# Deformable convolutions and a mixture of experts: where the token rows are normalised, and how often they are stored

## Chip, core and metric

The kernel runs on one core of a Trainium2 chip. Its time is the device time of one execution in microseconds; the time before is 7508.25 us, the median of three runs (7496.17 to 7528.83). The core has five engines with instruction queues of their own: TensorE (PE, with its weight loads PEld), VectorE (DVE), ScalarE (ACT), GpSimd (POOL) and SyncE (SP). SP and POOL issue the transfers here, SP the plain ones and POOL the indirect gathers.

## What is computed

Four images of 256 channels and 64 x 64 pixels, in float32, pass one block of two halves:

```python
# half 1: three deformable 3x3 convolutions on the normalised channels, added to x
x = x + conv3(_ln_c(x))            # each: offsets and mask by a 3x3 convolution,
                                   # 9 taps sampled bilinearly, times the mask, einsum, relu
# half 2: mixture of experts on tokens (a pixel is a token of 256 channels)
t = _to_tokens(x)                  # [4, 4096, 256]
z = (t - mean(t)) / sqrt(var(t) + 1e-5)          # over the channels of a token
probs = softmax(z @ gate_w + gate_b)             # 8 experts, the best two count
t = t + sum over e of cw[:, e] * (gelu(z @ W1[e] + b1[e]) @ W2[e] + b2[e])   # 256 -> 512 -> 256
x = _from_tokens(t)
```

A token goes to two of the eight experts. The kernel sorts the tokens by expert and computes only these.

## The kernel before

**The main work.** A stage is one convolution layer of one image; `run` lists the twelve stages. A stage has 8 blocks of 512 pixels, a block 9 taps. For each tap `samples` (L494) makes POOL gather four tables of corners (L503, 512 KB each, 10 buffers), DVE interpolates (L509, L514) and ACT multiplies by the mask (L517). `turn` transposes two such tiles on PE (L532) and ACT copies the result (L535); `finish` multiplies with the tap's weights (L555). `LAG` keeps the transposes two pairs behind the samples.

**The token path.** After the third layer `tokens` (L587) runs for each of the 32 blocks, cut by `yield` into pieces that are spread over the taps of the next block. It adds x (L599), transposes to tokens (L608, L613), multiplies with the gate (L618), stores the tokens `t` to DRAM (L626, 512 KB), computes mean and 1/sqrt(var) in `normalise` (L62 to L75), normalises the rows on DVE into `z` (L78, four instructions of 128x256), stores `z` (L636, 512 KB) and then ranks the experts (L645 to L686). Row r of a group's `z` table is token r: partition p and quarter t of a block hold token 128 t + p.

**The experts.** Tokens are handled in five groups: images 0, 1 and 2 as a whole, image 3 in two halves. `route` (L690) counts and makes slots, `invert` (L768) makes for each expert slot the number of its token, by a matmul with `self.token`. Then each tile of 256 slots goes through `expert` (L825) in three pieces: (1) `products` of the tile before (DVE adds the bias, L892, and SP stores the result, L895), four transposes of the gathered rows on PE (L840) and a copy on ACT (L844); (2) the first matmul (L856) and the Gelu on ACT (L866); (3) the second matmul (L874). `fetch` (L790) gathers the next tile's expert weights (L800, skipped for a repeated expert) and its token rows `zt` (L812, two gathers of 128 rows); it is called in piece 3, or in piece 2 while `draining`. There are two weight buffers and two buffers for each half of `zt`. There are 163 tiles in all.

**The sums.** `combine_load` (L902) reads tokens back from the `t` store, 128 partitions with two tokens each, `combine_fetch` (L915) gathers the two expert results of a token, `combine` (L930) adds them, weighted, and `give` transposes back and stores the output.

**What sets the order.** Three lanes (`routes`, `tiles`, `sums`) hold pieces with a price in taps. After each tap `pump` gives every lane one tap of credit, and a lane runs the pieces that its credit pays for. An expert tile costs `pace` taps: 5 for the groups of images 0 and 1, 2 for image 2, 1.5 for the first half of image 3, 0 for the second half, each piece a third of it. Where no taps are left, `settle` (between dependent stages and at the end) runs side pieces one by one with `drain(1)` beside each, and the end of `run` calls `drain(3)` until all lanes are empty. `drain(n)` runs n tile pieces and gives the other lanes n/3 and 2n/3 taps. The program's order of instructions is afterwards scheduled per engine ahead of time; `self.after(x)` keeps an instruction behind x in that order, and what has no such ordering may be moved forward to where its inputs are expected.

Of the kernel before, what the change touches and what calls it, by code (L numbers as in the profile page):

```python
# [8 lines left out]
F32 = mybir.dt.float32  # L9
I32 = mybir.dt.int32  # L10
AF = mybir.ActivationFunctionType
ALU = mybir.AluOpType
AX = mybir.AxisListType

P = 128
H = W = 64
C = 256
# [3 lines left out]
TPB = 4  # L21
BLK = P * TPB
NB = H * W // BLK
# [14 lines left out]
GB = 10  # L38
LAG = 2
LEAST = 2.0**-30  # L40
WINN = CC * (RPB + 2) * W
W1N = CC * HID + HC
W2N = HC * C + C
EPS_C = 1e-6
EPS_T = 1e-5
# [72 lines left out]
class Weave:  # L118
# [91 lines left out]

    def ffn_constants(self):
        nc, cst, ins = self.nc, self.cst, self.ins
        self.t_dram = [
            [
                self.dram.tile([P, TPB, C], F32, name=f"t_{b}_{n}", tag=f"t_{b}_{n}")
                for n in range(NB)
            ]
            for b in range(self.B)
        ]
        nf = max(g.NF for g in self.groups)  # L220
        for g in self.groups:
            g.zd = self.dram.tile([g.M * P, C], F32, name=f"z_{g.nm}", tag=f"z_{g.nm}")
        self.ys = [
            self.dram.tile([nf * FT, C], F32, name=f"ys_{i}", tag=f"ys_{i}") for i in range(3)
        ]
        self.gw = cst.tile([P, CC, E], F32, name="gw")
        nc.sync.dma_start(self.gw, ins["gate_w"].rearrange("(c p) e -> p c e", p=P))
        self.gb = cst.tile([P, E], F32, name="gb")
        nc.sync.dma_start(self.gb, ins["gate_b"])

        self.gsum = cst.tile([P, E], F32, name="gsum")

        self.before = cst.tile([P, E, E], F32, name="before")
        nc.vector.memset(self.before, 0.0)
        for e in range(1, E):
            nc.vector.memset(self.before[:, e, 0:e], 1.0)
        self.ones = cst.tile([P, P], F32, name="ones")
        nc.vector.memset(self.ones, 1.0)
        gp = self.ps.tile([P, E], F32, tag="tp", name="gp")
        for c in range(CC):  # L240
            nc.tensor.matmul(
                gp, lhsT=self.ones, rhs=self.gw[:, c, :], start=(c == 0), stop=(c == CC - 1)
            )
        nc.vector.tensor_copy(self.gsum, gp)

        self.upper = cst.tile([P, P], F32, name="upper")
        nc.gpsimd.affine_select(
            self.upper, self.ones, pattern=[[1, P]], base=0, channel_multiplier=-1,
            compare_op=ALU.is_gt, fill=0.0,
        )  # L250

        self.fresh = {}
        for M in {g.M for g in self.groups}:
            fresh = cst.tile([P, E, M], F32, name=f"fresh_{M}")
            nc.vector.memset(fresh, 1.0)
            nc.vector.memset(fresh[:, :, 0:1], 0.0)
            self.fresh[M] = fresh
        part_i = cst.tile([P, 1], I32, name="part_i")
        nc.gpsimd.iota(part_i, pattern=[[0, 1]], base=0, channel_multiplier=1)
        self.part = cst.tile([P, 1], F32, name="part")  # L260
        nc.vector.tensor_copy(self.part, part_i)

        row_i = self.big.tile([P, P], I32, tag="hv", name="row_i")
        nc.gpsimd.iota(row_i, pattern=[[1, P]], base=0, channel_multiplier=0)
        self.row_f = cst.tile([P, P], F32, name="row_f")
        nc.vector.tensor_copy(self.row_f, row_i)
        assert FU * nf <= P
        self.token = cst.tile([P, NB * TPB], F32, name="token")
        nc.vector.tensor_scalar(
            self.token, self.row_f[:, : NB * TPB], float(P), self.part, ALU.mult, ALU.add  # L270
        )


        self.w = None
# [312 lines left out]
    def tokens(self, b, n, r):  # L587

        nc = self.nc
        nm = f"tok_{b}_{n}"  # L590
        grp = next(g for g in self.groups if g.b == b and g.n0 <= n < g.n1)
# [6 lines left out]
        with self.after(self.last):  # L598
            nc.vector.tensor_tensor(r, r, xc, ALU.add)  # L599
        yield  # L600
        tok = self.big.tile([P, TPB, C], F32, tag="b", name=f"t_{nm}")
        z = self.big.tile([P, TPB, C], F32, tag="b", name=f"z_{nm}")
        lg = self.small.tile([P, TPB, E], F32, tag="lg", name=f"lg_{nm}")
        for t0 in range(0, TPB, 2):
            tp = self.ps.tile([P, 2, C], F32, tag="tp", name=f"tp_{nm}_{t0}")
            for t in range(2):
                for o in range(CC):
                    nc.tensor.transpose(  # L608
                        tp[:, t, o * P : (o + 1) * P],
                        r[:, o, (t0 + t) * P : (t0 + t + 1) * P],  # L610
                        self.ident,
                    )
            nc.scalar.copy(tok[:, t0 : t0 + 2, :], tp)  # L613

        lp = self.ps.tile([P, TPB, E], F32, tag="tp", name=f"lp_{nm}")
        for t in range(TPB):
# [6 lines left out]
                    stop=(c == CC - 1),  # L623
                )
        nc.scalar.copy(lg, lp)
        nc.sync.dma_start(self.t_dram[b][n], tok)  # L626
        yield
        rest = normalise(nc, self.small, tok, z, EPS_T, nm)
        with self.after(self.last):
            mean = next(rest)  # L630
            rs = next(rest)
        yield
        with self.after(self.last):
            next(rest, None)
        r0 = (n - grp.n0) * BLK
        nc.sync.dma_start(  # L636
            grp.zd[r0 : r0 + BLK, :].rearrange("(t p) c -> p t c", p=P), z
        )

        def small(tag, shape):  # L640
# [149 lines left out]
    def fetch(self, grp, step):  # L790

        if self.w is None:
            self.w = [
                self.wt.tile([P, 2, WINN], F32, tag="wt", name=f"w_{i}").rearrange(
                    "p a b -> p (a b)"
                )
                for i in range(2)
            ]
        f = grp.order[step]
        self.nc.gpsimd.indirect_dma_start(  # L800
            out=self.w[step % 2][:, : W1N + W2N],
            out_offset=None,
            in_=self.ins["W"],
            in_offset=bass.IndirectOffsetOnAxis(ap=grp.wrow[:, f : f + 1], axis=0),
            bounds_check=E * P - 1,
            oob_is_err=False,
        )
        grp.zt[step] = []
        for u in range(FU):
            zt = self.ffn.tile([P, C], F32, tag=f"zt{u}", name=f"zt_{grp.nm}_{f}_{u}")  # L810
            j = FU * f + u
            self.nc.gpsimd.indirect_dma_start(  # L812
                out=zt,
                out_offset=None,
                in_=grp.zd,
                in_offset=bass.IndirectOffsetOnAxis(ap=grp.tok[:, j : j + 1], axis=0),
            )
            grp.zt[step].append(zt)
# [6 lines left out]
    def expert(self, grp, step):  # L825

        nc = self.nc
        if step == 0:
            self.fetch(grp, 0)
            yield  # L830
        self.products(grp)
        f = grp.order[step]
        nm = f"{grp.nm}_{f}"
        w = self.w[step % 2]
        w1, w2 = w[:, :W1N], w[:, W1N : W1N + W2N]
        zt = grp.zt.pop(step)
        tp = self.ps.tile([P, CC, FT], F32, tag="tp", name=f"ftp_{nm}")
# [61 lines left out]

    def combine_load(self, grp, n, t0):  # L900
        a = self.ffn.tile([P, 2, C], F32, tag="c", bufs=3, name=f"ta_{grp.nm}_{n}_{t0}")
        self.nc.sync.dma_start(a, self.t_dram[grp.b][grp.n0 + n][:, t0 : t0 + 2, :])  # L902
        grp.acc.append(a)

    def combine_fetch(self, grp, m):
# [62 lines left out]
    def begin(self, grp):  # L968
        for step in range(grp.NF):
            gen = self.expert(grp, step)  # L970
            for _ in range(3 + (step == 0)):
                self.tiles.put(grp.pace / 3, lambda gen=gen: next(gen, None))
        self.tiles.put(grp.pace / 3, lambda: self.products(grp))
        self.tiles.put(3, lambda: self.end(grp))

# [36 lines left out]
    def settle(self):  # L1012
        while self.side or self.plans_side:
            for side in (self.side, self.plans_side):
                if side:
                    next(side.pop(0), None)
            if self.tiles.pieces:
                self.drain(1)
        self.draining = False

    def drain(self, pieces):

        self.draining = True
        for _ in range(pieces):
            if self.tiles.pieces:
                self.tiles.pop()
        if self.tiles.pieces:
            self.routes.go(pieces / 3)
            self.sums.go(2 * pieces / 3)
        elif self.routes.pieces:  # L1030
            self.routes.pop()
        elif self.sums.pieces:
            self.sums.pop()

    def run(self):
# [48 lines left out]
                self.finish()  # L1084
                self.settle()
        while self.routes.pieces or self.tiles.pieces or self.sums.pieces:
            self.drain(3)


# [46 lines left out]
```

## Time and profile before

| | |
|---|---|
| median of three runs | 7508.25 us |
| the profiled execution | 7520.62 us, of which the span of instructions is 7518.9 us |
| mean granted TensorE clock | 0.944 |
| PE / DVE / ACT / POOL busy | 86% / 66% / 43% / 60% |
| moved by DMA | 2223.73 MB, 296 GB/s on the mean |
| stages with tokens (third layer of images 0 to 3) | about 1620 to 2110, 3260 to 3850, 5080 to 5650, 6420 to 7090 us |
| experts beside the stages | 2305 to 7090 us, in four groups with pauses |
| end: last routing, last expert tiles, last sums | 7090 to 7519 us |

Lines are read in this way: a group is named by its line, engine, operation and tiles, with its count, its busy time, the mean duration of one, and the idle time of the engine just before it with what ended that. A line of the waits says which instruction sat waiting, and for whom: total time, number of times, the longest. A line of the chain gives the share of each engine in the work that ended last. In a timeline the columns are the start, the duration, engine, line, operation, tiles, the number of instructions merged, and in brackets the idle time ahead.

### The profile page before, as it was taken

To read this page: it belongs to the slowest core of one execution; us is meant where nothing else is said; L and a number is where in the kernel's file an instruction comes from. 1 tells how busy PE (TensorE), PEld (TensorE's weight loads), DVE (VectorE), ACT (ScalarE), POOL (GpSimd) and SP (SyncE) were. 2 spreads that over 40 slices of the span, in tenths; PEclk is the share of its full clock that TensorE was granted. 3 is DMA by queue.
4 is the path that set the end of the run, shared out by engine and by line. 5 is a ranking of instruction groups with operands and counts; after the bars stand their busy time and mean duration, and the time that the engine had idled before them with its cause. 6 is when DMAs were issued, how large, how long until landed. Compare 5 with 4: busy or idle time off the path is not lost.

```text
span 7518.9 us, 88985 instructions
## 1 busy us (share of the span) xinstructions
PE 6443.2 (86%) x26500; PEld 3618.8 (48%) x26500; DVE 4952.9 (66%) x11467; ACT 3266.0 (43%) x7141; POOL 4476.5 (60%) x4245
## 2 busy tenths in 40 slices
PE   6898888888898888889988888888888788977887
PEld 3443333334454444445554445444544555644565
DVE  6776777768887666567777556666768554667421
ACT  3444544445544444445443434444444333444322
POOL 4654666656666565556557656555656565666543
PEclk8999999999999999999999999999999899989998
DMA  8997999989998888888888888888888777888644
GB/s 266 337 325 274 352 342 335 346 331 356 362 349 311 300 305 297 278 315 322 314 293 316 293 280 314 295 302 294 308 306 299 251 271 240 288 302 287 211 139 123
DMA packets 800320, 2223.73 MB, mean 296 GB/s; under 512 B 104729, under 2 KB 302873, under 8 KB 794081
## 3 DMA queue, kind: packets, MB, share of 16 engines
q0 software_dynamic: 551200, 1947.35, 73.3%
q1 hardware_dynamic: 248640, 270.69, 10.9%
q8 instruction: 215, 3.52, 0.2%
q14 instruction: 265, 2.16, 0.1%
HBM read 2160.68 MB, written 196.40 MB: 313 GB/s over the span
## 4 chain that ended last, share of the span: by engine, by line
PE 69%; ACT 10%; issue 7%; another core or an unknown queue 6%; DVE 4%; DMA 2%; POOL 1%; SPq 0%; ACTq 0%; DVEq 0%; POOLq 0%
PE acc L555 34%; PE tp L532 10%; PE ph L856 7%; PE py L874 6%; PE po L357 6%; ACT sT L535 4%; ACT s L517 3%; DVE g L509 2%; DVE s L514 1%; PE pm L371 1%; ACT hT L866 1%; PE ftp L840 1%; ACT win L577 1%; PE tpv L325 1%
## 5 line engine op out<-in xcount | busy, mean ns | idle before, releaser
L503 POOL DMA_INDIRECT g<-tab,idx x3456 | 3685.4, 1066 | 2371.6 <-DVE s L514 1061.8
L555 PE MATMUL acc<-sT,wk 128*128 128x512 f32 x6912 | 3492.1, 620 | 253.4 <-ACT sT L535 147.5
L509 DVE SCALAR_TENSOR_TENSOR g<-g,cf 128x512 f32<-128x512 f32 x3456 | 2559.2, 742 | 269.1 <-DMA g<-tab,idx 245.5
L514 DVE SCALAR_TENSOR_TENSOR s<-g,cf 128x256 f32<-128x256 f32 x3456 | 1662.7, 483 | 1331.3 <-PE tp L532 729.9
L535 ACT COPY sT<-tp 128x512 f32<-128x512 f32 x1728 | 1002.0, 585 | 2312.0 <-PE tp L532 1553.0
L517 ACT ACTIVATE s<-s,cf 128x256 f32<-128x256 f32 x3456 | 1629.5, 508 | 256.7 <-DVE s L514 160.7
L555 PEld LDWEIGHTS acc<-sT,wk 128*128 128x128 f32 x6912 | 1198.9, 198 | 1106.7 <-issue 816.7
L532 PEld LDWEIGHTS tp<-ident,s 128*128 128x128 f32 x6912 | 893.2, 146 | 1666.2 <-issue 898.9
L532 PE MATMUL tp<-ident,s 128*128 128x128 f32 x6912 | 1287.3, 286 | 439.2 <-ACT s L517 253.8
L856 PE MATMUL ph<-fzT,w 128*128 128x256 f32 x2608 | 720.8, 411 | 78.0 <-ACT fzT L844 28.1
L874 PE MATMUL py<-w,hT 128*128 128x256 f32 x2608 | 671.1, 396 | 103.5 <-ACT hT L866 58.0
L856 PEld LDWEIGHTS ph<-fzT,w 128*128 128x128 f32 x2608 | 506.3, 205 | 212.9 <-issue 69.6
L874 PEld LDWEIGHTS py<-w,hT 128*128 128x128 f32 x2608 | 484.5, 196 | 242.0 <-issue 91.9
L866 ACT ACTIVATE hT<-ph,w 128x256 f32<-128x256 f32 x652 | 281.9, 471 | 616.3 <-PE ph L856 378.2
L812 POOL DMA_INDIRECT zt<-z,tok x326 | 333.8, 1024 | 161.5 <-issue 88.0
L800 POOL DMA_INDIRECT w<-in_W,wrow x163 | 178.0, 1092 | 381.2 <-issue 138.8
L357 PE MATMUL po<-win,wo 128*32 128x504 f32 (+1 forms) x2304 | 366.0, 615 | 6.5 <-ACT win L301 4.2
L892 DVE TENSOR_TENSOR y<-py,w 128x512 f32<-128x512 f32 x163 | 111.9, 686 | 341.5 <-PE py L874 285.1
L915 POOL DMA_INDIRECT gy<-ys,slots x256 | 255.6, 998 | 104.5 <-issue 70.0
L930 DVE SCALAR_TENSOR_TENSOR ta<-gy,cw,ta 128x256 f32<-128x256 f32 x256 | 120.6, 480 | 125.6 <-DMA gy<-ys,slots 78.4
L357 PE MATMUL po<-win_pre,wo 128*32 128x504 f32 (+1 forms) x1152 | 184.2, 617 | 2.0 <-ACT om L366 2.0
L366 ACT ACTIVATE om<-po,bo 128x512 f32<-128x512 f32 x96 | 65.9, 687 | 265.3 <-PE po L357 156.3
(154 smaller groups left out, 2961.0 us busy)
## 6 DMA issues: line engine op xcount, KB each, us to landing
tab<-hv SPq DMA_DIRECT2D x512, 128.0 KB
g<-tab,idx POOLq DMA_INDIRECT x3456
ys<-y SPq DMA_DIRECT2D x163, 256.0 KB
tab<-h_pre SPq DMA_DIRECT2D x128, 256.0 KB
wk<-in_conv_w SPq DMA_DIRECT2D x99, 256.0 KB
xc_pre<-in_x SPq DMA_DIRECT2D x32, 512.0 KB
xr_tok<-in_x SPq DMA_DIRECT2D x32, 512.0 KB
t<-t_tok SPq DMA_DIRECT2D x32, 512.0 KB
```

What stands on the lines that cost most here:

```text
L357: nc.tensor.matmul(po[g * Q : (g + 1) * Q, :].rearrange("q (r w) -> q r w", w=W)[:, :, x0:x1], lhsT=self.wo[l][:, 3 * ky + kx, c, :], rhs= ...
L503: self.gathered = nc.gpsimd.indirect_dma_start(out=g.rearrange("p x s f -> p (x s f)"), out_offset=None, in_=self.table(*self.stages[i]), ...
L509: nc.vector.scalar_tensor_tensor(g[:, :, 0, :], g[:, :, 1, :], cf[:, j, 0:1], g[:, :, 0, :], ALU.mult, ALU.add,)
L514: self.last = nc.vector.scalar_tensor_tensor(s, g[:, 1, 0, :], cf[:, j, 1:2], g[:, 0, 0, :], ALU.mult, ALU.add)
L517: nc.scalar.activation(s, s, AF.Copy, scale=cf[:, j, 2:3])
L532: self.turned = nc.tensor.transpose(tp[:, c, u * P : (u + 1) * P], ss[u][:, c * P : (c + 1) * P], self.ident)
L535: nc.scalar.copy(self.sT[:, :, t0 * P : (t0 + 2) * P], tp)
L555: nc.tensor.matmul(acc[:, o, :], lhsT=self.wk[k][:, c, o * P : (o + 1) * P], rhs=sT[:, c, :], start=(k == 0 and c == 0), stop=(k == K - 1 ...
L812: self.nc.gpsimd.indirect_dma_start(out=zt, out_offset=None, in_=grp.zd, in_offset=bass.IndirectOffsetOnAxis(ap=grp.tok[:, j : j + 1], axi ...
L856: nc.tensor.matmul(ph[:, h, :], lhsT=w1[:, o : o + P], rhs=zT[:, c, :], start=(c == 0), stop=(c == CC - 1),)
L866: nc.scalar.activation(ht[:, h, :], ph[:, h, :], AF.Gelu, bias=w1[:, k : k + 1])
L874: nc.tensor.matmul(py[:, u, :], lhsT=hT[h // 2][:, h % 2, u * P : (u + 1) * P], rhs=w2[:, h * C : (h + 1) * C], start=(h == 0), stop=(h == ...
```

## The change

The tokens of a block are stored once, in rows of 258 numbers: 256 channels, then 1/sqrt(var + eps) and -mean/sqrt(var + eps). There is one table per group in place of the `t` tiles and the `z` table. DVE writes the two numbers into the row; the four normalising instructions on DVE and the second store fall away. The row order becomes token 4 p + t, so a partition's four rows are one run of 4128 B, and `self.token` is made by an iota. The expert tiles gather these rows, 1032 B each, and a piece of its own, ahead of the transposes, normalises both halves in place on ACT (Identity with scale and bias per partition); `products` of the tile before moves with the transposes to the piece after it. An expert tile has four pieces in place of three, priced a quarter of `pace` each. `settle` calls `drain(2)`, the end `drain(4)`, and `drain(n)` gives n/4 and 2n/4 taps. `combine_load` reads the first 256 numbers of the rows. The token tile has a tag of its own with one buffer, where `t` and `z` shared two buffers with the pre-blocks' `h`.

```diff
@@ -38,6 +38,7 @@
 GB = 10
 LAG = 2
 LEAST = 2.0**-30
+ROW = C + 2
 WINN = CC * (RPB + 2) * W
 W1N = CC * HID + HC
 W2N = HC * C + C
@@ -210,16 +211,9 @@
 
     def ffn_constants(self):
         nc, cst, ins = self.nc, self.cst, self.ins
-        self.t_dram = [
-            [
-                self.dram.tile([P, TPB, C], F32, name=f"t_{b}_{n}", tag=f"t_{b}_{n}")
-                for n in range(NB)
-            ]
-            for b in range(self.B)
-        ]
         nf = max(g.NF for g in self.groups)
         for g in self.groups:
-            g.zd = self.dram.tile([g.M * P, C], F32, name=f"z_{g.nm}", tag=f"z_{g.nm}")
+            g.td = self.dram.tile([g.M * P, ROW], F32, name=f"t_{g.nm}", tag=f"t_{g.nm}")
         self.ys = [
             self.dram.tile([nf * FT, C], F32, name=f"ys_{i}", tag=f"ys_{i}") for i in range(3)
         ]
@@ -266,9 +260,11 @@
         nc.vector.tensor_copy(self.row_f, row_i)
         assert FU * nf <= P
         self.token = cst.tile([P, NB * TPB], F32, name="token")
-        nc.vector.tensor_scalar(
-            self.token, self.row_f[:, : NB * TPB], float(P), self.part, ALU.mult, ALU.add
-        )
+        token_i = self.big.tile([P, NB, TPB], I32, tag="hv", name="token_i")
+        nc.gpsimd.iota(
+            token_i, pattern=[[BLK, NB], [1, TPB]], base=0, channel_multiplier=TPB
+        )
+        nc.vector.tensor_copy(self.token, token_i.rearrange("p n t -> p (n t)"))
 
 
         self.w = None
@@ -598,8 +594,7 @@
         with self.after(self.last):
             nc.vector.tensor_tensor(r, r, xc, ALU.add)
         yield
-        tok = self.big.tile([P, TPB, C], F32, tag="b", name=f"t_{nm}")
-        z = self.big.tile([P, TPB, C], F32, tag="b", name=f"z_{nm}")
+        tok = self.big.tile([P, TPB, ROW], F32, tag="t", bufs=1, name=f"t_{nm}")
         lg = self.small.tile([P, TPB, E], F32, tag="lg", name=f"lg_{nm}")
         for t0 in range(0, TPB, 2):
             tp = self.ps.tile([P, 2, C], F32, tag="tp", name=f"tp_{nm}_{t0}")
@@ -610,7 +605,7 @@
                         r[:, o, (t0 + t) * P : (t0 + t + 1) * P],
                         self.ident,
                     )
-            nc.scalar.copy(tok[:, t0 : t0 + 2, :], tp)
+            nc.scalar.copy(tok[:, t0 : t0 + 2, :C], tp)
 
         lp = self.ps.tile([P, TPB, E], F32, tag="tp", name=f"lp_{nm}")
         for t in range(TPB):
@@ -623,18 +618,19 @@
                     stop=(c == CC - 1),
                 )
         nc.scalar.copy(lg, lp)
-        nc.sync.dma_start(self.t_dram[b][n], tok)
-        yield
-        rest = normalise(nc, self.small, tok, z, EPS_T, nm)
+        yield
+        rest = normalise(nc, self.small, tok[:, :, :C], None, EPS_T, nm)
         with self.after(self.last):
             mean = next(rest)
             rs = next(rest)
-        yield
-        with self.after(self.last):
-            next(rest, None)
+            nc.vector.tensor_copy(tok[:, :, C], rs)
+            nc.vector.scalar_tensor_tensor(
+                tok[:, :, C + 1], mean, -1.0, rs, ALU.mult, ALU.mult
+            )
+        yield
         r0 = (n - grp.n0) * BLK
         nc.sync.dma_start(
-            grp.zd[r0 : r0 + BLK, :].rearrange("(t p) c -> p t c", p=P), z
+            grp.td[r0 : r0 + BLK, :].rearrange("(p t) c -> p t c", p=P), tok
         )
 
         def small(tag, shape):
@@ -807,12 +803,12 @@
         )
         grp.zt[step] = []
         for u in range(FU):
-            zt = self.ffn.tile([P, C], F32, tag=f"zt{u}", name=f"zt_{grp.nm}_{f}_{u}")
+            zt = self.ffn.tile([P, ROW], F32, tag=f"zt{u}", name=f"zt_{grp.nm}_{f}_{u}")
             j = FU * f + u
             self.nc.gpsimd.indirect_dma_start(
                 out=zt,
                 out_offset=None,
-                in_=grp.zd,
+                in_=grp.td,
                 in_offset=bass.IndirectOffsetOnAxis(ap=grp.tok[:, j : j + 1], axis=0),
             )
             grp.zt[step].append(zt)
@@ -828,6 +824,12 @@
         if step == 0:
             self.fetch(grp, 0)
             yield
+        for zt in grp.zt[step]:
+            nc.scalar.activation(
+                zt[:, :C], zt[:, :C], AF.Identity,
+                scale=zt[:, C : C + 1], bias=zt[:, C + 1 : C + 2],
+            )
+        yield
         self.products(grp)
         f = grp.order[step]
         nm = f"{grp.nm}_{f}"
@@ -899,7 +901,8 @@
 
     def combine_load(self, grp, n, t0):
         a = self.ffn.tile([P, 2, C], F32, tag="c", bufs=3, name=f"ta_{grp.nm}_{n}_{t0}")
-        self.nc.sync.dma_start(a, self.t_dram[grp.b][grp.n0 + n][:, t0 : t0 + 2, :])
+        rows = grp.td[n * BLK : (n + 1) * BLK, :].rearrange("(p t) c -> p t c", p=P)
+        self.nc.sync.dma_start(a, rows[:, t0 : t0 + 2, :C])
         grp.acc.append(a)
 
     def combine_fetch(self, grp, m):
@@ -968,8 +971,8 @@
     def begin(self, grp):
         for step in range(grp.NF):
             gen = self.expert(grp, step)
-            for _ in range(3 + (step == 0)):
-                self.tiles.put(grp.pace / 3, lambda gen=gen: next(gen, None))
+            for _ in range(4 + (step == 0)):
+                self.tiles.put(grp.pace / 4, lambda gen=gen: next(gen, None))
         self.tiles.put(grp.pace / 3, lambda: self.products(grp))
         self.tiles.put(3, lambda: self.end(grp))
 
@@ -1015,7 +1018,7 @@
                 if side:
                     next(side.pop(0), None)
             if self.tiles.pieces:
-                self.drain(1)
+                self.drain(2)
         self.draining = False
 
     def drain(self, pieces):
@@ -1025,8 +1028,8 @@
             if self.tiles.pieces:
                 self.tiles.pop()
         if self.tiles.pieces:
-            self.routes.go(pieces / 3)
-            self.sums.go(2 * pieces / 3)
+            self.routes.go(pieces / 4)
+            self.sums.go(2 * pieces / 4)
         elif self.routes.pieces:
             self.routes.pop()
         elif self.sums.pieces:
@@ -1084,7 +1087,7 @@
                 self.finish()
                 self.settle()
         while self.routes.pieces or self.tiles.pieces or self.sums.pieces:
-            self.drain(3)
+            self.drain(4)
 
 
 def kernel(**inputs):
```

## Prediction

> **What bounds the kernel now.** I read the page from the top: busy shares, then the chain that ended last, then the costliest groups, and after that the waits and the windows of single stages.
>
> ```profile
> PE 6443.2 (86%) x26500; PEld 3618.8 (48%) x26500; DVE 4952.9 (66%) x11467; ACT 3266.0 (43%) x7141; POOL 4476.5 (60%) x4245
> ...
> PE 69%; ACT 10%; issue 7%; another core or an unknown queue 6%; DVE 4%; DMA 2%; POOL 1%; SPq 0%; ACTq 0%; DVEq 0%; POOLq 0%
> ```
>
> TensorE is busy for 86% of the span and holds 69% of the chain. ScalarE has much free time (43% busy), but 10% of the chain; VectorE holds 4% and DMA 2%. Work taken from DVE or DMA is therefore mostly work taken from beside the path, and work given to ACT is partly on it.
>
> The change touches three kinds of stages, and they differ. The windows are: a stage with tokens and the next image's pre-blocks (1630 to 2110), a stretch with experts at pace 2 (5920 to 6340), and the final drain (7390 to 7466). The columns are PE, PEld, DVE, ACT and POOL busy, then the granted clock, DMA share and GB/s.
>
> ```profile
> 1630.00:2110.00 480.00, 422.43 (x1738) 221.19 (x1735) 412.66 (x1113) 241.49 (x529) 302.01 (x275) 0.95 0.96 353
> 5920.00:6340.00 420.00, 375.38 (x1607) 243.56 (x1607) 221.90 (x442) 166.91 (x379) 248.89 (x248) 0.96 0.78 264
> ...
> 7390.00:7466.00 76.00, 72.17 (x328) 58.09 (x326) 6.44 (x10) 19.39 (x45) 16.96 (x18) 1.00 0.29 87
> ```
>
> In the first, PE (88%), DVE (86%) and DMA (96%) are all close to full: here alone is relief of DVE and DMA worth something. In the second DVE and ACT are half idle. In the third PE is 95% busy, one expert tile per 8.2 us (the bias additions of L892 come 8.2 us apart), with ACT 26% busy.
>
> What ends the waits of DVE in the pace-2 stretch:
>
> ```profile
> DVE g L509 <- DMA g<-tab,idx: 130.6, 34, 10.9
> ...
> POOL w L800 <- ACT sT L535: 75.9, 11, 18.2
> ```
>
> POOL holds the weight fetch back (its buffer comes free with L892 two tiles back; in the trace L800 there starts 1.5 us after L892), the tap gathers stand behind it in POOL's queue, and DVE waits for them. One such place, POOL's queue by time:
>
> ```profile
> 6118.46 1.36 POOL L800 DMA_INDIRECT w<-in_W,wrow  x1 [4.07 <-ACT sT L535]
> 6120.12 1.35 POOL L812 DMA_INDIRECT zt<-z,tok  x1 [0.30 <-issue]
> 6121.78 0.98 POOL L812 DMA_INDIRECT zt<-z,tok  x1 [0.30 <-issue]
> ...
> 6125.60 0.95 POOL L503 DMA_INDIRECT g<-tab,idx  x1 [0.30 <-issue]
> ```
>
> The gather issued at 6125.60 is first used at 6129.99 on DVE: 4.4 us from POOL to landing under this load.
>
> **The change, part by part.** The sum is made against the profiled execution, 7520.6 us (span 7518.9); the median shown, 7508, is 12 us below it, and I scale the result by that at the end.
>
> *DVE in the token blocks.* Removed: the normalising group and nothing else on DVE.
>
> ```profile
> L78 DVE TENSOR_SCALAR z_tok<-t_tok,mv_tok,rs_tok 128x256 f32<-128x256 f32 x128 | 45.8, 417 | 0.4
> ```
>
> Added: two 128x4 instructions per block, like L73 at 0.16 us: 64 x 0.16 = 10.2 us. Net -35.6 us of DVE, 1.1 us in each of 32 blocks. Hidden today behind PE in most stages; bounds 0 and -36. The chain of the window 1630 to 2110 gives DVE 9% (L509 4.8, L514 3.9), elsewhere 4%; a quarter of the blocks lies there. The burst also delays the two operations behind it, so I take somewhat more than those shares: **-6 us**.
>
> *Stores, queues of SP and DMA.* One store of 4128 B per partition replaces two of 512 KB; 32 issues of 0.36 us leave SP's queue, where nothing waits for them. The z rows were 1 KB packets: 16384 of them, 50 ns each in the trace's DMA records, over 16 engines 51 us. Given back: the combine loads (L902) read 1 KB runs instead of 2 KB (16384 x 50 ns instead of 8192 x 96 ns, +2 us), and the gathered rows are 1032 B. The gathers of 1 KB rows stand in the records as 4 KB packets (four rows, 184 ns); if rows of 1032 B go singly, 41728 x 50 ns against 10432 x 184 ns is +10 us. Net -39 us of DMA time, bounds -51 and +12 on the path. DMA holds 2% of the chain, and the first window is 96% full, where 8 of 32 blocks lie (8/32 x 39 = 10 us at most). I take **-6 us**.
>
> *Normalising on ACT.* 326 instructions of 128x256 with scale and bias per partition. The nearest rows are L517 (scale per partition, 508 ns) and L866 (bias per partition, 471 ns): 326 x 0.508 = 166 us. No table load is added: the Identity of L366 carries none, while L866 and L661 show 23 and 22 loads of 1.28 us. Most lies beside PE. Bounds 0 and +166; with ACT's share of the chain, 10%, **+17 us**. If the cover went, each tile would cost 1.0 us.
>
> Against this move speaks the Trainium skill (ScalarE: Activation LUTs, "Rules for kernel authors" and "What ACT_TABLE_LOAD costs"): multiplications and additions belong on VectorE, and each per-partition pointer adds some 93 ns to 186 + 0.833 N ns. For one pointer that is 492 ns, beside the 508 and 471 of this trace; for two 585 ns, 191 us in all, and the term would be 19 us instead of 17. The rule compares engines, but here the row that counts is which engine is free: in the first window DVE is 86% busy and ACT 50%.
>
> *The added wait.* ACT now waits for the gather, where PE waited before. Behind it in ACT's order stand L517, L535 and L866, and PE waits for all three. How far ahead is the gather? Lanes advance once per tap. Counted out with the credits of the code, at pace 5 the fetch comes two taps before the transposes, before and after; the new piece falls one tap after the fetch. In the trace the transposes start 28 to 48 us after the second zt gather at that pace, so one tap (about 8 us) earlier leaves 20 us: no wait. At pace 2 the fetch and the new piece fall into the same tap, one tap before the transposes; lead there 11 to 30 us, less 8, against 4.4 us to landing and a weight fetch ahead of it. ACT is idle there in any case, since the next samples wait for their own gathers, issued later. 49 tiles run at pace 2 or 1.5; bounds 0 and 49 x 4.4 = +216 us; I take 0.2 us each, near the lower end because the gather that ends DVE's wait is the later one: **+10 us**.
>
> *The pieces.* At paces 5 and 2 the bias addition and the next weight fetch keep their distance (3 taps and 1 tap). At pace 1.5 half of the tiles have them in one tap instead of one tap apart, so POOL loses its lead: some 6 tiles, bounds 0 and +50 (a tap each), taken as **+8 us**. At the settling of stage 10 twelve side steps take 24 pieces of four to the tile instead of 12 of three: 6 tiles instead of 4. PE is full there (9.6 to 10 of 10 us in most slices of 6360 to 6410), and stage 11 runs at much the same pace with a tile (a bias addition every 17.2 us, two taps) as without (L599 every 74 us, nine taps): 2 x 8.2 = 16 us at most, I take +6. At the last settling 1.2 tiles more stand ahead of the last group's routing, in a stretch (7100 to 7190) that has 15 us of idle PE: 0 to -15, I take -5. Together **+1 us**.
>
> *The final drain.* Per tile 1.0 us on an ACT that is busy for a quarter; where a gather is late (L840 waits for zt 4 times in all, 7.2 us), the new step is added. Bounds 0 and +33 (33 tiles); **+2 us**.
>
> Sum: -6 - 6 + 17 + 10 + 8 + 1 + 2 = +26 us, 0.35%. On the median: **7534 us**, inside 0.5%, which is about what a measurement of this kernel can tell from no change.
>
> **The rivals.**
>
> *A, slower: ACT is stopped by the gather at every tile.* The instruction order is set ahead of time, and operations without an ordering are put where their inputs were expected: L647, one piece later in the program than the z operations of L78, ran 5 us before them, in the middle of the chain for rs.
>
> ```profile
> 6767.80 0.16 DVE L68 TENSOR_SCALAR ve_tok<-mv_tok 128x4 f32<-128x4 f32 x1
> 6767.87 0.18 DVE L647 TENSOR_TENSOR pr_tok<-gsum,mv_tok 128x32 f32<-128x32 f32 x1
> ...
> 6772.99 1.38 DVE L78 TENSOR_SCALAR z_tok<-t_tok,mv_tok,rs_tok 128x256 f32<-128x256 f32 x4
> ```
>
> The new ACT instructions have no ordering either; they may stand right where the gather was expected, and wait up to 4.4 us. For it: the unordered memset L290 makes DVE wait up to 14.7 us. Against: DVE runs ahead of PE (L514 waits 730 us for PE), so a stop of some us is covered. It decides from the point where the wait exceeds that lead. With 0.6 us exposed per tile, 163 x 0.6 = 98 us: 7508 + 98 = 7606 us; fully exposed ACT work (+166) gives 7674.
>
> *B, faster: the token stages were held by DVE and DMA.* Then the 36 us of DVE and most of the DMA time count and ACT hides all: about -55 us, 7453 us. For it: the first window's 86% and 96%. Against: that holds for one token stage in four; in the others DMA is at 0.85 to 0.89.
>
> *C, nothing is seen:* all of it is covered, 7508 us; it lies in my forecast's own class.
>
> **How the numbers follow.** Forecast and C together 0.44, A 0.38 (all of it slower by over 0.5%), B 0.18. The range leaves out the ends of A and of B: 7455 to 7650. Faster 0.18, within 0.5% 0.44, slower 0.38.
>
> **What would show it.** Right: ACT busy near 3430 us, DVE near 4917, hardly any idle time of the new instruction on DMA zt, PE's wait for L517 near 254 us, stage lengths unchanged to a per cent. Wrong: a group of waits of the new instruction on zt of 100 us or more with PE's waits for L517, L535 and L866 grown beside it (A); or the stretch 1600 to 2110 shortened by 10 us or more and the other token stages too (B).

## The result and the profile after

The changed kernel takes 7556.62 us (median of six runs, 7544.25 to 7561.1), the kernel before 7503.91 us in runs beside it: ratio 1.0067, 95% interval 1.005 to 1.0084. It is slower by 38 to 63 us. The forecast of 7534 us stood for "within 0.5%"; the time lies 23 us above it, inside the range, but in the class "slower". The profiled execution took 7561.1 us (span 7559.4), 40.5 us more than the one of before.

The groups of runs met two conditions, one in which the kernel before needs about 7505 us (as in the result) and one in which it needs about 6803 us; I call them the slow and the fast condition (the recorded texts say chip, but the record has the same chip number, 14, beside a group of either kind, so what makes them is not known) and compare only within a group, as a ratio.

From the page of the changed kernel, the busy line and two groups (operation, tiles, shapes, count, then busy us, mean ns, and the idle time just before with its releaser):

```profile
PE 6460.3 (85%) x26500; PEld 3631.3 (48%) x26500; DVE 4921.8 (65%) x11403; ACT 3438.5 (45%) x7465; POOL 4475.3 (59%) x4246
...
L894 DVE TENSOR_TENSOR y<-py,w 128x512 f32<-128x512 f32 x163 | 111.9, 687 | 413.7 <-PE py L876 353.4
...
L828 ACT ACTIVATE zt<-zt 128x256 f32<-128x256 f32 x326 | 182.3, 598 | 104.5 <-DMA zt<-t,tok 103.2
```

DVE has lost 31 us of work and ACT has gained 172, near the 36 and 166 worked out. The new instruction takes 598 ns, not the 508 ns of the one-pointer row. Here the rule of the Trainium skill (ScalarE: Activation LUTs, "What ACT_TABLE_LOAD costs") was the nearer, with an estimate of 585 ns for two pointers. The new instruction waits 104 us for its gather, 80 of them in the last 450 us.

The windows of the changed kernel: the token stage shown in the prediction, then the whole stage (1,3) with the settling behind it (first gather to the first gather of the next stage), then the drain. Columns as in the prediction.

```profile
1630.00:2110.00 480.00, 424.04 (x1737) 221.26 (x1736) 411.95 (x1113) 244.10 (x533) 309.84 (x279) 0.94 0.94 347
5608.00:6428.00 820.00, 679.78 (x2735) 414.42 (x2734) 445.17 (x987) 336.83 (x731) 443.10 (x433) 0.91 0.74 249
7430.00:7506.00 76.00, 72.18 (x329) 58.46 (x328) 6.22 (x9) 25.16 (x56) 17.42 (x18) 1.00 0.29 87
```

The same stage (1,3) in the kernel before:

```profile
5625.00:6391.00 766.00, 656.97 (x2742) 409.84 (x2741) 445.61 (x994) 307.43 (x675) 451.08 (x431) 0.93 0.78 266
```

The token stage and the drain are as they were. Stage (1,3), the one with experts at pace 2, is 54 us longer with the second matmul of 26 expert tiles in both. PE is busy there for 23 us more, at a lower granted clock (0.91 against 0.93), and idle for 31 us more. At its start the changed kernel was 17 us ahead (5608 against 5625), at its end it is 37 us behind. So the question is one stage. What DVE waits for there, before and after (us in total, times, longest; "remote" as the releaser means that the trace of this core names none):

```profile
DVE g L509 <- DMA g<-tab,idx: 138.1, 37, 10.9
DVE y L892 <- PE py L874: 44.9, 9, 7.7
...
DVE s L514 <- remote: 15.2, 6, 6.8
```

```profile
DVE y L894 <- PE py L876: 96.6, 14, 9.3
DVE g L505 <- DMA g<-tab,idx: 60.1, 28, 6.3
DVE s L510 <- remote: 34.5, 9, 9.8
...
DVE y L894 <- remote: 26.0, 8, 3.9
```

And the weight fetch on POOL, before and after. Its buffer comes free with an earlier y, though the trace names other instructions as the last to release it:

```profile
POOL w L800 <- ACT sT L535: 75.9, 11, 18.2
...
POOL w L800 <- issue: 18.8, 7, 7.3
```

```profile
POOL w L796 <- ACT sT L531: 87.2, 12, 21.7
...
POOL w L796 <- ACT o L957: 55.1, 5, 16.6
```

DVE waits less for gathers (60 us against 138) and more for the second matmul of the expert tile (97 and 26 us against 45), and POOL stands longer at the next weight fetch. The new instruction's own wait there is 20.0 us in 4 places.

### The profile page after: what moved, and what is told of

Read it like the earlier page. It is cut to its first block, busy times and chain, and to the rows that moved or that the text cites. A ratio compares the mean times of both kernels' runs of the same rounds, so it can differ in the third digit from the quotient of the medians.

```text
span 7559.4 us, 89230 instructions
## 1 busy us (share of the span) xinstructions
PE 6460.3 (85%) x26500; PEld 3631.3 (48%) x26500; DVE 4921.8 (65%) x11403; ACT 3438.5 (45%) x7465; POOL 4475.3 (59%) x4246
## 5 line engine op out<-in xcount | busy, mean ns | idle before, releaser
L499 POOL DMA_INDIRECT g<-tab,idx x3456 | 3686.5, 1067 | 2341.5 <-DVE s L510 938.1
L551 PE MATMUL acc<-sT,wk 128*128 128x512 f32 x6912 | 3500.3, 620 | 237.7 <-ACT sT L531 128.7
L528 PE MATMUL tp<-ident,s 128*128 128x128 f32 x6912 | 1287.1, 286 | 451.8 <-ACT s L513 272.6
L808 POOL DMA_INDIRECT zt<-t,tok x326 | 329.0, 1009 | 189.0 <-issue 103.0
L828 ACT ACTIVATE zt<-zt 128x256 f32<-128x256 f32 x326 | 182.3, 598 | 104.5 <-DMA zt<-t,tok 103.2
```

The costliest lines, as they stand in the source:

```text
L499: self.gathered = nc.gpsimd.indirect_dma_start(out=g.rearrange("p x s f -> p (x s f)"), out_offset=None, in_=self.table(*self.stages[i]), ...
L528: self.turned = nc.tensor.transpose(tp[:, c, u * P : (u + 1) * P], ss[u][:, c * P : (c + 1) * P], self.ident)
L551: nc.tensor.matmul(acc[:, o, :], lhsT=self.wk[k][:, c, o * P : (o + 1) * P], rhs=sT[:, c, :], start=(k == 0 and c == 0), stop=(k == K - 1 ...
L808: self.nc.gpsimd.indirect_dma_start(out=zt, out_offset=None, in_=grp.td, in_offset=bass.IndirectOffsetOnAxis(ap=grp.tok[:, j : j + 1], axi ...
```

## The experiments

Theory **N**: normalising on ACT costs this time. Theory **P**: the fourth piece puts the expert's instructions in a worse order. Theory **S**: the settling, now 56 us instead of 42, is lost time. Theory **R** came later: the loss depends on pauses that only the slow condition has. The stage times below go from the first gather of (1,3) to the first gather of (2,3), read from the timeline of L503/L499.

### Settling with one piece (fast condition)

```diff
-                self.drain(2)
+                self.drain(1)
```

> The changed kernel, with one piece instead of two to each side step at the settling, so that four tiles stand there as before the change (three, rounded by pieces of four). The settling after stage (1,3) took 56 us in the changed kernel's trace against 42 us. Theory S (the two tiles more at the settling are lost time): 14 us less than the changed kernel, about 7543 us. Theory N (the normalising on ScalarE lengthens stage (1,3)) and theory P (the fourth piece sets the experts' instructions in a worse order beside the taps of stage (1,3)): the tiles moved out of the settling cost the same later, within 5 us of the changed kernel, about 7557 us; the stage (1,3) still takes some 764 us from its first to its last gather.

Measured: 6790.9 us, ratio to before 0.9986 (0.9977 to 0.9995); stage 666 us.

### Normalising inside the transposing piece, three pieces (fast condition)

```diff
-        yield
         self.products(grp)
...
-            for _ in range(4 + (step == 0)):
-                self.tiles.put(grp.pace / 4, lambda gen=gen: next(gen, None))
+            for _ in range(3 + (step == 0)):
+                self.tiles.put(grp.pace / 3, lambda gen=gen: next(gen, None))
```

and the settling, the drain and the credits as before the change (the normalising loop now stands directly ahead of `products`).

> The changed kernel with the normalising at the head of the piece that transposes, and with three pieces to a tile, paces and settling as before the change. All of the new ScalarE work and the single store stay. Theory P: the 40 us of stage (1,3) and the 14 us of the settling go, and the 17 us gained up to that stage stay: about 7490 us, stage (1,3) 724 us from first to last gather. Theory N: the same work on the same engine, now even nearer to the transposes that need it: about 7555 us, stage (1,3) 760 us or more. Theory S: the settling's 14 us alone go, about 7543 us.

Measured: 6792.89 us, ratio 0.9984 (0.9975 to 0.9993); stage 697 us.

### The kernel before with an empty fourth piece (fast condition)

```diff
         if step == 0:
             self.fetch(grp, 0)
             yield
+        yield
         self.products(grp)
```

with four pieces, quarters of the pace, `drain(2)` and `drain(4)`.

> The kernel before with an empty fourth piece at the same place, a quarter of the pace to each piece and two pieces to a side step: pacing and settling of the change alone, with no new instruction, two stores, rows of 1 KB. Theory P: slower than the kernel before by 45 to 60 us (no gain of the token blocks to set against it), about 7555 us. Theory N: unchanged, about 7504 us. Theory S: about 14 us slower, 7518 us.

Measured: 6788.07 us, ratio 0.9978 (0.9969 to 0.9987); stage 665 us.

### The changed kernel without the normalising (fast condition)

```diff
-        for zt in grp.zt[step]:
-            nc.scalar.activation(
-                zt[:, :C], zt[:, :C], AF.Identity,
-                scale=zt[:, C : C + 1], bias=zt[:, C + 1 : C + 2],
-            )
         yield
```

> The changed kernel with the normalising instructions of the expert tiles left out (the experts then work on rows that are not normalised); its piece stays, empty, with the pacing and the settling of the change. Theory N: the loss goes and the gain of the token blocks stays: about 7490 us. Theory P: about 7545 to 7555 us, stage (1,3) still 760 us. Theory S: 7557 less what the instructions cost on the path by my forecast (17 + 10 us), about 7530 us, with the settling still 56 us.

Measured: 6776.83 us, ratio 0.9963 (0.9949 to 0.9977); stage 666 us.

These four fit none of N, P and S: every one is faster than the kernel before, by 0.14% to 0.37%, the fourth piece alone too. The condition was the other one. The windows of stage (1,3) there, first of the kernel with three pieces and the normalising inside, then of the kernel before with four:

```profile
5072.00:5768.00 696.00, 636.74 (x2736) 399.57 (x2735) 444.12 (x989) 344.51 (x730) 449.02 (x431) 0.96 0.84 292
```

```profile
5081.00:5746.00 665.00, 626.10 (x2740) 397.01 (x2739) 452.67 (x991) 310.70 (x676) 451.88 (x431) 0.97 0.88 309
```

In the fast condition the kernels with four pieces have this stage 31 us shorter than the one with three, where four had seemed to lengthen it; the kernel before has no trace there. In the whole kernel less is left of it: with the normalising in place, four pieces (0.9986, one piece at the settling) and three (0.9984) take the same time. S is not borne out in this condition: one piece at the settling leaves the stage at 666 us, as two do; the tiles not done there turn up later (stage (2,3) 597 against 614 us in the run without the normalising, the end behind it 446 against 420).

### Once more, beside each other: the changed kernel, the kernel before, and two places for the normalising (slow condition)

> The changed kernel itself once more, because the chip of the first four experiments ran the kernel before in 6802 us where the chip of the prediction's result needed 7504. What I call theory R: on the slow chip a large part of the time is idle time of ScalarE and VectorE for which the trace names no releaser of this core (868 us in all in the kernel before, ScalarE's sT, hT and om and VectorE's s alone 800); the loss of 50 us is a matter of where those stops fall, and on a chip without them the changed kernel is no slower: ratio 0.996 to 1.000. Theories N and P: the loss belongs to the instruction stream and is there on either chip: ratio 1.003 or more. If this run lands on a chip like the first, its ratio is again 1.005 to 1.008.

Measured: 7564.44 us, ratio 1.0088 (1.0068 to 1.0108); stage 827 us.

> The kernel before itself, for a trace on the chip that the other runs of this batch share. Ratio 1.000. Theory R on a fast chip: no stops without a releaser, and the stage (1,3) with its settling lasts 30 us longer than in the kernel with the empty fourth piece (three pieces to a tile then are the slower order, as the 697 us against 666 us of the second and third experiment suggest). Theory P: it is 30 us shorter than there.

Measured: ratio 1.0019 (0.9997 to 1.004); stage 762 us.

On VectorE:

```diff
         for zt in grp.zt[step]:
-            nc.scalar.activation(
-                zt[:, :C], zt[:, :C], AF.Identity,
-                scale=zt[:, C : C + 1], bias=zt[:, C + 1 : C + 2],
-            )
+            with self.after(self.last):
+                nc.vector.tensor_scalar(
+                    zt[:, :C], zt[:, :C], zt[:, C : C + 1], zt[:, C + 1 : C + 2],
+                    ALU.mult, ALU.add,
+                )
         yield
```

> The changed kernel with the gathered rows normalised on VectorE (one multiplication and addition with a pointer each, ordered behind the newest sample) instead of ScalarE. Theory N: ScalarE's 0.6 us ahead of the samples' scale and the transposes is what costs; VectorE is idle for a third and takes it for nothing: 8 to 14 us less than the changed kernel in the same batch. Rival D: VectorE stands still for the gather of the rows and its samples queue behind it: 10 us or more above the changed kernel.

Measured: 7555.91 us, ratio 1.0083 (1.0065 to 1.0102); stage 823 us.

At the head of the second of four pieces (the `yield` moved ahead of the loop):

> The changed kernel with the normalising at the head of the piece that transposes; the first piece stays, empty, so that pacing, settling and work are those of the change and only the place of the new instructions moves, by a quarter of a tile's pace. If their early place costs (a wait for the gather with samples behind it): 5 to 15 us less than the changed kernel in the same batch. If their work or the pacing costs: within 5 us of it. If an own piece hides their latency from the transposes: 5 to 15 us more.

Measured: 7564.34 us, ratio 1.008 (1.0056 to 1.0105); stage 826 us.

N falls for nearly all of the loss: on ACT early, on ACT late and on DVE the stage is within 4 us of the same length. On DVE the whole is 8.5 us shorter than on ACT, the low end of what N forecast, but the intervals overlap and some 54 us of the loss stay. The loss belongs to what these three share, in this condition: the four pieces with their settling, or the longer rows with the single store. The traces then showed what the pieces do. In stage (1,3) the order of instructions on PE in the changed kernel agrees with that of the fourth piece alone to 0.98, with that of the kernel before to only 0.66; the kernel with three pieces agrees with before to 0.99. The late variant (0.87 with the changed kernel) and the one on DVE (0.81) have orders of their own, nearer to the changed kernel than to before (0.66 and 0.60).

### Three of them again

> The kernel before with the empty fourth piece and the change's settling once more (the third experiment), since the second batch ran on a chip like that of the result, where the changed kernel took 1.0088 and its stage (1,3) with the settling 827 us against 762. Here too I compare within the batch. If the chip is again the slow one (the kernel before near 7500 us): theory P, the four pieces put the experts' instructions where the pauses of that chip stop TensorE: stage (1,3) 815 to 830 us, ratio 1.007 to 1.012 (the loss of 60 us with no gain of the token blocks). Theory N or the longer rows: 760 to 775 us, ratio 0.999 to 1.003. On the fast chip: 0.998 again.

Measured, in the fast condition: 6786.72 us, ratio 0.9973 (0.9962 to 0.9983); stage 666 us. It repeats the third run and leaves the slow condition open.

> The changed kernel with the normalising inside the piece that transposes, three pieces, paces and settling as before the change, once more (the second experiment). On the slow chip, theory P: the loss in stage (1,3) goes (762 to 775 us) and the gain of the token blocks stays: ratio 0.996 to 1.000. Theory N or the longer rows: stage (1,3) stays at 815 us or more, ratio 1.006 to 1.009. A third case, both orders are bad there (on the fast chip this one's stage was the longer, 697 us against 666): 780 to 810 us and a ratio of 1.001 to 1.005. On the fast chip: 0.998 again.

Measured, in the fast condition: 6793.37 us, ratio 0.9982 (0.9973 to 0.9991); stage 699 us.

> The same kernel as in the second and eighth run: normalising inside the piece that transposes, three pieces, paces and settling as before the change; single store, longer rows and new ScalarE work all kept. The traces of the runs so far show that TensorE's order in it is nearly that of the kernel before (0.98 of its stage (1,3) agrees), while the changed kernel and the kernel with only the fourth piece share another one (0.64 agrees with before). If this run lands on the slow chip: theory P (the order made by four pieces loses 60 us there): stage (1,3) with its settling 760 to 780 us, ratio 0.996 to 1.001. The rows of 1032 B, the store or the normalising: 810 to 830 us, ratio 1.006 to 1.009. On the fast chip: 0.998 again, 697 us, and nothing new.

Measured, in the slow condition: 7490.44 us, ratio 0.9983 (0.9969 to 0.9997); stage 764 us. The windows of stage (1,3), of the changed kernel in the slow condition (second execution), then of this one:

```profile
5602.00:6429.00 827.00, 678.53 (x2731) 416.32 (x2730) 444.99 (x986) 336.69 (x730) 445.66 (x433) 0.90 0.73 247
```

```profile
5572.00:6336.00 764.00, 652.84 (x2732) 406.22 (x2731) 442.76 (x988) 333.78 (x730) 449.75 (x431) 0.93 0.77 266
```

Store, rows of 1032 B and the normalising on ACT are all there. Only the four pieces, with the settling and the credits that belong to them, are undone, and the 63 us are gone. The longer rows and the store fall as a cause by themselves, and P holds in the slow condition; how much of it is the settling, 57 us there against 48, was not taken apart. The loss also depends on the condition: nearly the order of the changed kernel (0.99, one piece at the settling) took 0.9986 in the fast one, where the changed kernel itself was not run. That the pauses of theory R make this difference is not shown.

> The kernel before with the empty fourth piece and the change's settling, for the one cell that is still open: the four pieces alone on the slow chip. There undoing them in the changed kernel has just given 0.9983 in place of 1.0088. If they alone make the loss (theory P): 1.007 to 1.012, stage (1,3) with its settling 815 to 830 us. If it takes them together with the normalising or the longer rows: 1.000 to 1.005, 765 to 800 us. On the fast chip: 0.9975 again, 665 us, and the cell stays open.

Measured, in the fast condition: 6785.29 us, ratio 0.9976 (0.9967 to 0.9985). Nothing new: that the four pieces alone, without the rest of the change, lose in the slow condition was not measured.

### What the order does

For the 19 expert tiles inside stage (1,3), read from the timeline (medians, us): the period from one bias addition y to the next, and how long y starts behind the end of its second matmul py.

```
                                     cond.  stage  period  y behind py
before (second execution)            slow    762    20.3      4.1
three pieces, normalising inside     slow    764    20.1      4.1
changed kernel                       slow    820    23.5      0.0
changed kernel (second execution)    slow    827    23.9      0.0
normalising on DVE                   slow    823    24.5      0.0
normalising late                     slow    826    24.6      0.0
three pieces, normalising inside     fast    697    19.6      9.7
before with a fourth piece           fast    665    18.0      4.2
changed, one piece at the settling   fast    666    17.9      3.7
```

With three pieces y starts some 4 to 6 us further behind py. In the fast condition both orders have some time left, and the tighter one has the shorter stage. In the slow condition the looser order still has 4 us, while in the tighter one y starts at the end of py (0.0): DVE arrives first and stands still for y, with what comes behind it in its order, and the weight buffer comes free later. The waits of DVE in that stage, of the changed kernel (second execution) and of the three-piece kernel, both in the slow condition (line numbers of the variants are off by one or two):

```profile
DVE y L894 <- PE py L876: 94.3, 14, 9.4
DVE g L505 <- DMA g<-tab,idx: 78.1, 39, 5.4
DVE s L510 <- remote: 57.0, 13, 11.0
...
DVE y L894 <- remote: 20.0, 6, 3.8
```

```profile
DVE g L505 <- DMA g<-tab,idx: 133.7, 44, 10.3
DVE y L893 <- PE py L875: 42.1, 9, 7.8
...
DVE s L510 <- remote: 16.9, 7, 5.8
...
DVE y L893 <- remote: 4.0, 6, 1.1
```

For y it is 114 against 46 us: the difference, 68 us, is of the size of the loss, but that proves little, since the waits for gathers fall by 56 us at the same time and those for s without a named releaser rise by 40. Of the stage's 63 us PE is busy for 26 more, at a clock of 0.90 against 0.93, and idle for 37 more. That the pieces with their settling make the loss there is shown by undoing them; that y is the link is read from the traces and was not tried by moving y alone.

## Why the prediction was right in its range and wrong in its class

- **What bounds it, and where:** right that little is held by DVE and DMA. "Stage lengths unchanged to a per cent" was wrong for one stage in twelve: (1,3) +7%; the others moved by at most 2.2%, and two executions of one kernel differ by up to 1.8% in a stage.
- **DVE and the stores (-6 and -6):** about right, as far as can be seen. In the fast condition the fourth piece alone gives 0.9978 and the fourth piece with the single store, without normalising, 0.9963: 0.15% of 6803 us, 10 us, with intervals that overlap (0.9969 to 0.9987, 0.9949 to 0.9977). In the result's trace 17 us had been gained by 5608 us, which is hardly clear of noise: kernels with the same store start that stage between 5572 and 5621 us.
- **Normalising on ACT (+17), the wait for zt (+10), the drain (+2):** too dear, at least in the slow condition. With three pieces, where all of it is in place beside the single store, the kernel is 0.17% faster than before (13 us; 2 to 23), where my terms without the pieces and the settling sum to +17. In the fast condition, the changed kernel with one piece at the settling stands at 0.9986 and the one without normalising at 0.9963: up to 16 us for 182 us of work, the settling's difference included. The ACT wait of 104 us is there, but 80 us of it lie in the last 450 us, where ACT is busy for a third of the time.
- **The pieces (+8) and the settling (+1):** the step that failed. "At paces 5 and 2 the bias addition and the next weight fetch keep their distance" looked at one distance and by it charged pace 2 with nothing; the loss sits at pace 2. What moved was the first matmul, the second matmul and y against each other. From the changed kernel's 1.0088 to the 0.9983 of three pieces it is 0.0105 x 7505 = 79 us (63 from the result's 1.0067), where I had 9. At the settling 14 us more are visible in the result's trace, within the bound of 16; in the fast condition one piece in place of two there moved tiles and left the stage as long.
- **The rivals:** A gave the right class by the wrong mechanism. Its first sign came, 104 us of waits for zt, but of PE's waits that were to grow beside it the one for L517 went from 253.8 to 272.6 us and the one for L535 fell from 147.5 to 128.7, and the loss stays when the work goes to DVE. B was wrong: the first token stage takes 496 us against 498 (and in the last one the DMA share is 0.81, below the 0.85 to 0.89 that I gave for the others). No rival had the order of the experts' pieces as its mechanism. So it was luck that the sum came near, by two errors that offset each other: some 30 us too dear for the normalising and the relief, 54 to 70 us too cheap for the pieces.

A version that is ahead of the kernel before in both conditions came out of it: one store, normalising on ACT inside the transposing piece, three pieces. It takes 0.9982 to 0.9984 of the time before in the fast condition and 0.9983 (0.9969 to 0.9997) in the slow one, where it also beats the changed kernel.

## What to carry to other kernels

When an added step gets a slot of its own in a hand-made pacing, the slot can cost more than the step: work out for every pace which instructions then fall into one tap, and how far each consumer stands behind its producer, not one such distance. Where an instruction is put close behind its producer, a few microseconds of slack may decide the sign; here that reading fits the traces but was not tried alone. And before a change of half a per cent is kept or dropped, measure it in both conditions in which the kernel runs: kernels with four pieces had one stage 31 us shorter in one and some 60 us longer in the other.

## What was not expected of the hardware

The two conditions differ by 10% on the same program (7505 and 6803 us), while DVE's and ACT's instructions take the same time (the multiplication by the mask, L517, 508 ns in both). What differs is the granted clock (0.944 and 0.979) and pauses. In the changed kernel's profile, around one slow tile:

```profile
5979.72 3.59 PE L353 MATMUL po<-win,wo 128*32 128x512 f32 x28
...
5986.91 0.99 POOL L499 DMA_INDIRECT g<-tab,idx  x1 [0.30 <-issue]
...
5991.14 0.69 ACT L362 ACTIVATE om<-po,bo 128x512 f32<-128x512 f32 x1 [10.89 <-remote]
...
5993.98 0.84 ACT L868 ACTIVATE hT<-ph,w 128x256 f32<-128x256 f32 x2 [1.75 <-remote]
5994.08 0.48 DVE L510 SCALAR_TENSOR_TENSOR s<-g,cf 128x256 f32<-128x256 f32 x1 [5.62 <-remote]
...
5994.87 3.78 PE L858 MATMUL ph<-fzT,w 128*128 128x256 f32 x8 [8.55 <-ACT hT L868]
```

The matmuls that om needs end at 5983.3 by the profile (its ends are modelled), but ACT starts 7.8 us later with "remote" as the releaser; DVE pauses too, while POOL goes on issuing gathers. In the timeline of the changed kernel ACT has 280 pauses of over 1.5 us that are put down to "remote" or "issue", 997 us in all, and the kernel before 282 with 1058 us; the kernel with the fourth piece in the fast condition has one, of 4 us. Of the pauses of the changed kernel's first execution 176 return in the second within two ACT instructions of the same place, where chance would give about 50. DMA doesn't stop in them: packets move at 329 GB/s against 292 on the mean, and PE is busy for 65% of their time. The slow traces also lack many updates of semaphores, by which a trace tells who released whom: in the changed kernel 8120 of 11232 of DVE, 4209 of 5175 of PE and 5177 of 7096 of ACT are there, in the fourth-piece kernel of the fast condition all but a few. So "remote" can stand for a release that was not recorded; the pause itself is in the times of the instructions.

The half-speed stretches of the PE clock are 839 us long in the changed kernel's second execution and 294 us in the fourth-piece kernel in the fast condition. But for one of about 50 us at the very end they come in multiples of 3.4 us, which agrees with what the Trainium skill (TensorE: Matmul & The Clock Gate, "What's actually happening") says of a window of about 3.4 us of idleness that halves the clock. In stage (1,3) in the slow condition they are 102 us for the kernel before and 160 us for the changed one (second executions), so a part of that stage's loss is slower matmuls. Whether the pauses bring these stretches about was not shown, and what makes the pauses is open.
